# Second layer of a two-layer network on one core: score products of 64 rows placed in both row halves of the array in turn, with `center` held twice

## The chip, the cores and the metric

The kernel runs on one core of one Trainium2 chip. The metric is device time in microseconds (us), the median of several executions; lower is better. One more execution was taken with the hardware profiler on. It gives the span of the program (first to last instruction) and a trace of every instruction, and all start times below are counted from the start of that span.

The engines are named as in the profile: PE is the matrix engine and PEld its weight loads, DVE, ACT and POOL are the three engines for vectors, SP issues most of the DMAs. [...]

## What is computed

Four images of 512 channels and 32x32 pixels go through two layers, each with a residual. The first layer (group norm, layer norm, a selective scan, a projection) isn't touched by the change. The second is attention over positions and two 3x3 convolutions, on the group-normed image:

```python
def _L1_conv_ref(x, w_top, b_top, w_center, b_center, w_bottom, b_bottom, w_out, b_out):
    B, C, OUT_C, PAB, H, W = (4, 512, 512, 64, 64, 64)
    ...
    x_top = _conv(x, w_top, b_top, 0).reshape(bsz, -1, hw)          # 64 x 1024
    x_center = _conv(x, w_center, b_center, 0).reshape(bsz, -1, hw) # 64 x 1024
    x_bottom = _conv(x, w_bottom, b_bottom, 1).reshape(bsz, c, hw)  # 3x3, 512 -> 512
    ...
    sp_map = jnp.einsum('bnp,bpm->bnm', x_center, x_top)            # 1024 x 1024 scores, sum over 64
    sp_map = jax.nn.softmax(sp_map.reshape(bsz, -1), axis=1).reshape(bsz, hw, hw)
    sp_map = jnp.einsum('bnm,bmc->bnc', sp_map, x_bottom)
    sp_map = sp_map.reshape(bsz, c, h, w)
    return _conv(x + sp_map, w_out, b_out, 1)                       # 3x3, 512 -> 512

x = x + _L0_conv_ref(_gn(x), ...)
x = x + _L1_conv_ref(_gn(x), ...)
```

The softmax runs over all 1024 x 1024 scores of an image at once. What matters here is that a score is a sum over only 64 products (`PAB = 64`), half of the 128 rows that the array has.

## The kernel before

**Two parts.** The first layer takes the span up to about 1872 us; there an order written by hand (`Plan`) issues the instructions. In the second layer the instructions are traced in plain Python order, and the framework's scheduler then fixes an order on each engine, puts in the waits and hands out the buffers of a pool to its tiles. An engine works through its own list strictly in order, so an instruction that waits holds up everything behind it on that engine. The scheduler's order need not be the traced one: work traced later is put into gaps.

**The calls for each image.** The functions are called in this order (the loop at the end of the kernel): `scores(0)`; then for images 0 and 1: `conv3(b0)`, `attend(0)`, `scores(1)`, `conv3(b1)`, `attend(1)`; then `conv3(o0)`, `finish(0)`, `conv3(o1)`, `finish(1)`, `scores(2)`, and the same for images 2 and 3. So there are four calls of `scores`, and behind each comes the 3x3 convolution `conv3(b...)` (`x_bottom`) of the same image, and only behind that `attend`, which needs the softmax.

**`scores`** makes the scores and their exponentials for one image:

- `top` and `center` (128x1024, in SBUF, from the pool `fp` under tag `f4` with three buffers, shared with the output tiles `o` of `finish`) get zeros in their rows 64 to 127 by two POOL memsets (L1406, L1407).
- For each half `h` of the positions, four fp32 matmuls (L1411, tile `pt`, weights of `top` and `center` side by side) give 64 rows of `top` and, in rows 64 to 127, 64 rows of `center`. ACT writes `center` (64x512, one instruction, L1416) and then `top` (four instructions of 64x128, L1423, which also put the positions into the order of the convolution's tiles).
- For each of eight groups `m` of 128 positions, and each half `h`, one fp32 matmul (L1432, tile `psc`) of 128 rows, of which 64 are the zeros. The profile shows each fp32 matmul as two passes, each with a weight load, so a call has 16 matmuls and 32 passes. ACT copies each result into `st` (L1436), DVE takes the row maximum of each 128x1024 `st` (L1437).
- A maximum over everything: DVE `mp` (L1440), POOL `ma` across the partitions (L1442), DVE negates it (L1443). Then eight exponentials of 128x1024 on ACT, in place (L1446), and their sum `rp` on DVE (L1450).

**`conv3`** is a 3x3 convolution in a transformed form: six row points `p` in the pairs (1, 2), (3, 4), (0, 5), and for each of them four column points `q` in the order 2, 1, 0, 3. A product is four matmuls (eight passes, L1584) into one tile `m`; for `p = q = 1` a matmul with one row adds the bias (L1589). Its weights (1 MB, tile `uw`, three buffers `u`) come by an SP DMA (L1580). DVE makes the inputs `v` (`rr` by L1483, L1484, L1547, L1556; then four instructions, L1461 to L1464), with help of ACT (`e`, `f`, L1480) and POOL (L1481, L1543, L1544, L1553, L1554). For each `p`, ACT scales `m[2]` into `e` (L1592) and DVE combines `m[1]`, `m[0]` and `m[3]` with it (L1601, four instructions). Only then is a bank of PSUM free again.

**Banks of PSUM.** The pool `pm` (tag `m`) has five, used by the `m` tiles of `conv3`; the pool `ps` (tag `ps`) has three, used by `pt`, `psc`, `pat` (`attend`), and the transposes `po` of `finish`. So PE can run five `m` tiles ahead of ACT and DVE in `conv3`.

**`attend`** multiplies the exponentials with `x_bottom` (L1643, 128 matmuls per image) and adds the result to the image (DVE, L1658). For images 0 and 1, DVE also transforms pieces of the second convolution's weights there (L1508 to L1519).

The lines that the change touches are the first half of `scores`:

Of the kernel before, what the change touches and what calls it, by code (L numbers as in the profile page):

```python
# [8 lines left out]
F32 = mybir.dt.float32  # L9
AF = mybir.ActivationFunctionType  # L10
ALU = mybir.AluOpType
AX = mybir.AxisListType
# [3 lines left out]
P = 128  # L16
B, C, HH, WW = 4, 512, 32, 32
L = HH * WW
# [5 lines left out]
T = 512  # L24
NH = L // T
NB = B * NH
PAB = 64
# [4 lines left out]
    xp=(1, 2, 1),  # L32
# [184 lines left out]
def mamba_then_pab_kernel(  # L217
# [25 lines left out]
    nc = tc.nc  # L243
# [20 lines left out]
    pb_sb = cpool.tile([P, 1], F32, tag="pb", name="pb_sb")  # L264
# [58 lines left out]
    with ExitStack() as l0:  # L323
# [985 lines left out]
        for b in range(B):  # L1309
            at = b * NDC * NS  # L1310
            for n in range(NDC):
                e, h = divmod(n, NH)
# [30 lines left out]
    with ExitStack() as l1:  # L1343

        pm = l1.enter_context(tc.tile_pool(name="l1pm", bufs=5, space=PSUM))
        ps = l1.enter_context(tc.tile_pool(name="l1ps", bufs=3, space=PSUM))
        wp = l1.enter_context(tc.tile_pool(name="l1w", bufs=1))

        TI, TJ = HH // 4, WW // 2
# [6 lines left out]
        xp = l1.enter_context(tc.tile_pool(name="l1x", bufs=2))  # L1356
        fp = l1.enter_context(tc.tile_pool(name="l1f", bufs=3))

        NMC = L // P
# [40 lines left out]
        def scores(b, xg):  # L1400

            top = fp.tile([P, L], F32, tag="f4", name=f"top_{b}")
            center = fp.tile([P, L], F32, tag="f4", name=f"center_{b}")
            nc.gpsimd.memset(top[PAB:P, :], 0.0)  # L1406
            nc.gpsimd.memset(center[PAB:P, :], 0.0)  # L1407
            for h in range(NH):
                pt = ps.tile([P, T], F32, tag="ps", name=f"pt_{b}_{h}")
                for c in range(NCC):  # L1410
                    nc.tensor.matmul(  # L1411
                        pt, wt_sb[:, c].rearrange("p j n -> p (j n)"),
                        xg[:, c, 1 + h * HR : 1 + (h + 1) * HR, 1 : WW + 1],
                        start=(c == 0), stop=(c == NCC - 1),
                    )
                nc.scalar.activation(  # L1416
                    center[0:PAB, h * T : (h + 1) * T], pt[PAB:P], AF.Identity, bias=pb_sb[PAB:P]
                )
                tv = top[0:PAB].rearrange("p (r k i j) -> p r i j k", r=4, k=2, j=TJ)
                pv = pt[0:PAB].rearrange("p (i r j k) -> p r i j k", r=4, j=TJ, k=2)  # L1420
                hi = slice(h * TI // 2, (h + 1) * TI // 2)
                for r in range(4):
                    nc.scalar.activation(  # L1423
                        tv[:, r, hi], pv[:, r], AF.Identity, bias=pb_sb[0:PAB]
                    )
            mx = spool.tile([P, NMC], F32, tag="mx", name=f"mx_{b}")
            st = []
            for m in range(NMC):
                t = xp.tile([P, L], F32, tag="st", name=f"st_{b}_{m}", bufs=NMC)
                for h in range(NH):  # L1430
                    pt = ps.tile([P, T], F32, tag="ps", name=f"psc_{b}_{m}_{h}")
                    nc.tensor.matmul(  # L1432
                        pt, top[:, m * P : (m + 1) * P], center[:, h * T : (h + 1) * T],
                        start=True, stop=True,
                    )
                    nc.scalar.copy(t[:, h * T : (h + 1) * T], pt)  # L1436
                nc.vector.reduce_max(mx[:, m : m + 1], t, axis=AX.X)  # L1437
                st.append(t)
            mp = spool.tile([P, 1], F32, tag="mp", name=f"mp_{b}")
            nc.vector.reduce_max(mp, mx, axis=AX.X)  # L1440
            ma = spool.tile([P, 1], F32, tag="ma", name=f"ma_{b}")
            nc.gpsimd.partition_all_reduce(ma, mp, P, bass_isa.ReduceOp.max)  # L1442
            nc.vector.tensor_scalar_mul(ma, ma, -1.0)  # L1443
            rs = spool.tile([P, NMC], F32, tag="rs", name=f"rs_{b}")
            for m in range(NMC):
                nc.scalar.activation(  # L1446
                    st[m], st[m], AF.Exp, bias=ma, accum_out=rs[:, m : m + 1]
                )
            rp = spool.tile([P, 1], F32, tag="rp", name=f"rp_{b}")
            nc.vector.reduce_sum(rp, rs, axis=AX.X)  # L1450
            return st, rp
# [310 lines left out]
        left = list(range(EARLY, NPC))  # L1762
        half = len(left) // 2
        st, rp = scores(0, image[0])
        for a in range(0, B, 2):
            ins = None
            for b in (a, a + 1):
                xb = conv3(f"b{b}", image[b], ub, brow[0], behind=ins)
                also = left[b * half : (b + 1) * half] if not a else []
                after, v = iter(()), None  # L1770
                if b == a:
                    after = norm(b + 1)
                    next(after)
                    next(after)
                else:
                    v = first_inputs(f"o{a}", image[a])
                ins = attend(b, image[b], st, rp, xb, after, also)
                if b == a:
                    st, rp = scores(b + 1, image[b + 1])
            if a + 2 < B:  # L1780
                after = norm(a + 2, True)
                mid = lambda: next(after)
            else:
                mid = None
            y = conv3(f"o{a}", image[a], uo, brow[1], v, mid=mid)
            next(after, None)
            finish(a, y)
            if a + 2 == B:
                last(a + 1, image[a + 1], None)
                break  # L1790
            next(after, None)
            finish(a + 1, conv3(f"o{a + 1}", image[a + 1], uo, brow[1]))
            st, rp = scores(a + 2, image[a + 2])
# [57 lines left out]
```

## Time and profile before

| what | us |
|---|---|
| median of 3 executions | 2886.27 (2882.78 to 2889.2) |
| the profiled execution, device time | 2896.7 |
| the profiled execution, span | 2894.9 |
| outside the span (2896.7 - 2894.9) | 1.8 |
| second layer, from the first instruction of `scores(0)` to the end | about 1022 |
| `psc` matmuls, PE busy, all four calls (128 passes) | 55.8 |
| copies `st<-psc`, ACT busy, all four calls (64) | 37.5 |
| row maxima `mx<-st`, 32 of 1.22 us | 39.0 |
| memsets of `top` and `center`, POOL, 8 of 0.95 us | 7.6 |

The groups of the profile give busy time, the mean of one instruction, and the idle time of the engine just ahead of them with what ended it. The chain of waits is followed back from the last instruction: what stands in it set the end of the program, and work that does not stand in it was hidden. The timeline shows instructions in order of time, equal neighbours merged; in square brackets is the idle time ahead, and what ended it.

The four calls of `scores` lie at these times on PE (start of the first `pt`, start of the first `psc`, end of the last):

| call | first `pt` | first `psc` | last `psc` ends | what PE does between `pt` and `psc` |
|---|---|---|---|---|
| `scores(0)` | 1875.80 | 1886.98 | 1900.95 | idle for 1.31 us |
| `scores(1)` | 2043.59 | 2053.36 | 2067.26 | 4 passes of `m_b`, with 0.93 us idle ahead |
| `scores(2)` | 2392.40 | 2403.86 | 2417.86 | passes of `m_b` and the bias, no idle time |
| `scores(3)` | 2553.16 | 2561.77 | 2575.67 | 4 passes of `m_b`, no idle time |

### The profile page before, as it was taken

How to read it: one execution, taken by the hardware profiler on the slowest of the kernel's cores; microseconds unless marked ns; L12 is line 12 of the kernel's file. 1: busy time of each engine (PE TensorE's matmuls, PEld its weight loads, DVE VectorE, ACT ScalarE, POOL GpSimd, SP SyncE). 2: the span in 40 equal slices, each digit the busy share in tenths (PEclk: the TensorE clock that was granted, in tenths of full speed). 3: DMA queues.
4: the chain of work that ended last, by engine and by line, in shares of the span. 5: the costliest groups of instructions: out<-in, count | busy, mean ns of one | idle time of the engine just before them, and what ended most of it. 6: DMA issues, size and time to landing. Idle time of an engine off the chain costs nothing.

```text
span 2894.9 us, 36258 instructions
## 1 busy us (share of the span) xinstructions
PE 2720.9 (94%) x11752; PEld 1628.6 (56%) x11752; DVE 2288.4 (79%) x2730; ACT 1837.1 (63%) x3250; POOL 2039.3 (70%) x1243
## 2 busy tenths in 40 slices
PE   6898799999999999989989999899999999999999
PEld 2466566666666666666667766544444444444445
DVE  4579999989999889989899999867776755346264
ACT  4789999999899999899999999530300003030000
POOL 6999999899998999999999999733241341214222
PEclk9999999999999999999999999899999999999999
DMA  6766655567655577645565664757789886536586
GB/s 182 209 178 190 190 166 176 159 216 243 197 163 167 161 230 229 200 144 179 160 203 178 210 196 147 180 215 259 257 277 304 315 322 240 188 123 240 189 318 241
DMA packets 406548, 603.68 MB, mean 209 GB/s; under 512 B 47224, under 2 KB 246136, under 8 KB 382040
## 3 DMA queue, kind: packets, MB, share of 16 engines
q1 hardware_dynamic: 398744, 587.11, 63.6%
q10 hardware_dynamic: 7616, 14.26, 1.3%
q8 instruction: 94, 1.54, 0.2%
q14 instruction: 94, 0.77, 0.1%
HBM read 504.27 MB, written 96.99 MB: 208 GB/s over the span
## 4 chain that ended last, share of the span: by engine, by line
PE 44%; ACT 19%; DVE 15%; POOL 9%; issue 6%; DMA 5%; SPq 0%; POOLq 0%; DVEq 0%; ACTq 0%
PE m_o L1584 10%; PE m_b L1584 8%; DVE da L957 5%; ACT sc L917 4%; PE y L990 4%; PE pat L1643 4%; ACT da L904 4%; PE u L943 3%; POOL da L980 3%; PE pxm L444 3%; PE po L444 3%; ACT u L904 3%; PE pz L444 2%; DVE u L957 2%; PE pp L800 1%
## 5 line engine op out<-in xcount | busy, mean ns | idle before, releaser
L980 POOL TENSOR_TENSOR da<-da,cbc 128x1024 f32<-128x1024 f32 x314 | 741.6, 2368 | 33.3 <-DVE da L957 8.3
L917 ACT ACTIVATE sc<-dtxt,bt_sb 128x256 f32<-128x256 f32 x1256 | 550.7, 499 | 17.1 <-PE u L943 16.4
L932 POOL TENSOR_TENSOR dbx<-dtx,bbc 128x1024 f32<-128x1024 f32 x198 | 467.1, 2369 | 20.2 <-PE y L990 7.8
L904 ACT ACTIVATE da<-dt,a_sb 128x512 f32<-128x512 f32 x628 | 433.7, 714 | 15.4 <-PE y L990 10.6
L957 DVE TENSOR_TENSOR_SCAN da<-da,u 128x512 f32<-128x512 f32 x328 | 383.1, 1203 | 40.5 <-PE u L943 23.3
L943 PE MATMUL u<-ident,sc 128*128 128x128 f32 x2512 | 363.1, 279 | 33.4 <-DVE da L957 19.6
L943 PEld LDWEIGHTS u<-ident,sc 128*128 128x128 f32 x2512 | 291.6, 142 | 161.6 <-issue 47.2
L957 DVE TENSOR_TENSOR_SCAN da<-da,carry_sb,u 128x512 f32<-128x512 f32 x300 | 367.2, 1260 | 13.7 <-PE u L943 10.3
L990 PE MATMUL y<-ident,da 128*128 128x128 f32 x2512 | 339.5, 277 | 27.7 <-POOL da L980 27.0
L1584 PE MATMUL m_b<-uw_b,v_b 128*128 128x512 f32 x768 | 335.2, 596 | 6.7 <-DMA uw_b<-u_b 4.4
L990 PEld LDWEIGHTS y<-ident,da 128*128 128x128 f32 x2512 | 290.3, 142 | 90.2 <-POOL da L980 49.0
L1584 PE MATMUL m_o<-uw_o,v_o 128*128 128x512 f32 x736 | 321.9, 596 | 4.2 <-DMA uw_o<-u_o 4.1
L904 ACT ACTIVATE u<-dt,a_sb 128x512 f32<-128x512 f32 x396 | 262.5, 681 | 10.7 <-DVE da L957 5.8
L444 PE MATMUL pxm<-xt,winc 128*128 128x345 f32 (+3 forms) x704 | 242.7, 488 | 18.6 <-DVE xs L706 4.7
L1584 PEld LDWEIGHTS m_b<-uw_b,v_b 128*128 128x128 f32 x768 | 145.5, 191 | 192.9 <-issue 178.6
L444 PE MATMUL pz<-xt,winc 128*128 128x512 f32 x512 | 240.3, 600 | 2.1 <-ACT dtxt L881 1.0
L1584 PEld LDWEIGHTS m_o<-uw_o,v_o 128*128 128x128 f32 x736 | 139.0, 191 | 180.2 <-issue 173.2
L990 PE MATMUL y<-ident,dbx 128*128 128x128 f32 x1584 | 219.8, 276 | 12.2 <-DVE dbx L973 7.1
L980 POOL TENSOR_TENSOR dbx<-dbx,cbc 128x1024 f32<-128x1024 f32 x91 | 215.2, 2365 | 13.8 <-DVE dbx L957 7.0
L1643 PE MATMUL pat<-y_b,st 128*128 128x512 f32 x512 | 221.6, 593 | 1.7 <-DVE rz L1654 1.6
L990 PEld LDWEIGHTS y<-ident,dbx 128*128 128x128 f32 x1584 | 182.6, 142 | 48.4 <-issue 22.1
L444 PE MATMUL po<-gt,wpr 128*128 128x512 f32 x384 | 182.4, 594 | 4.3 <-DVE u L957 2.3
(231 smaller groups left out, 4113.2 us busy)
## 6 DMA issues: line engine op xcount, KB each, us to landing
cbc<-bcd SPq DMA_DIRECT2D x512, 256.0 KB, 3.6
uw_b<-u_b SPq DMA_DIRECT2D x96, 1024.0 KB, 4.8
uw_o<-u_o SPq DMA_DIRECT2D x92, 1024.0 KB, 4.8
bbc<-bcd SPq DMA_DIRECT2D x198, 256.0 KB, 4.1
u_b<-work SPq DMA_DIRECT2D x192, 128.0 KB, 2.7
winc<-in_w_in_dram SPq DMA_DIRECT2D x72, 256.0 KB, 3.6
szd<-sz SPq DMA_DIRECT2D x32, 512.0 KB, 3.7
szl<-szd SPq DMA_DIRECT2D x32, 512.0 KB, 5.0
```

What stands on the lines that cost most here:

```text
L444: lambda k=k, lhs=lhs, rhs=rhs: nc.tensor.matmul(p()[:, at : at + cols], lhs(), rhs(), start=(k == 0), stop=(k == n - 1)),
L800: lambda d=d, hs=hs, pp=pp: nc.tensor.matmul(pp()[p0 : p0 + NP, :], wx_sb[:, d, :], xs[b, d]()[:, hs], start=(d == 0), stop=(d == NDC - 1),),
L904: nc.scalar.activation(t, dt()[:, j], AF.Exp, scale=a_sb[:, at : at + 1])
L917: nc.scalar.activation(sc()[:, k], dtxt()[:, k], AF.Copy, scale=bt[:, at, s : s + 1])
L932: lambda: nc.gpsimd.tensor_mul(hc(), dtx(), b_bc().to_broadcast([P, 2, T])),
L943: nc.tensor.transpose(u()[:, k * P : (k + 1) * P], sc()[:, k, j, :], ident)
L957: nc.vector.tensor_tensor_scan(ht, *((hc()[:, j], u()) if on_act else (u(), hc()[:, j])), carry_sb[:, j, s : s + 1] if h else 0.0, ALU.mul ...
L980: nc.gpsimd.tensor_mul(hc(), hc(), c_bc().to_broadcast([P, 2, T]))
L990: nc.tensor.matmul(y[j]()[:, k, :], hc()[:, j, k * P : (k + 1) * P], ident, start=(s == 0 and k == 0), stop=(s == NS - 1 and k == NK - 1), ...
L1584: nc.tensor.matmul(m[q], v[:, q, k, c, :], w[:, c, :], start=(c == 0), stop=(c == NCC - 1 and not extra),)
L1643: nc.tensor.matmul(pt, st[m][:, 2 * P * j + h : 2 * P * (j + 1) : 2], xb[m // 2][:, m % 2, :], start=(m == 0), stop=(m == NMC - 1),)
```

## The change

All of it is in `scores`.

- The two memsets go.
- `top` is held without zeros: its groups `m` of even number lie in rows 0 to 63, those of odd number in rows 64 to 127. Two ACT instructions of 64x256 write it for each `h`, one for each row half, in place of four of 64x128.
- `center` is written twice, into rows 0 to 63 and into rows 64 to 127, each by an ACT instruction of 64x512, and both now stand behind the instructions for `top`.
- The score matmuls contract over 64 rows instead of 128. They are issued in pairs: group `g` with rows 0 to 63, then group `g + 1` with rows 64 to 127, first for `h = 0`, then for `h = 1`. The first of a pair writes into a bank of `ps`, the second into one of `pm`. Number of matmuls, columns and copies stay as they are.
- The copies follow a pair at a time, and the two row maxima of a pair come behind its four copies.

```diff
             center = fp.tile([P, L], F32, tag="f4", name=f"center_{b}")
-            nc.gpsimd.memset(top[PAB:P, :], 0.0)
-            nc.gpsimd.memset(center[PAB:P, :], 0.0)
             for h in range(NH):
...
-                nc.scalar.activation(
-                    center[0:PAB, h * T : (h + 1) * T], pt[PAB:P], AF.Identity, bias=pb_sb[PAB:P]
-                )
-                tv = top[0:PAB].rearrange("p (r k i j) -> p r i j k", r=4, k=2, j=TJ)
-                pv = pt[0:PAB].rearrange("p (i r j k) -> p r i j k", r=4, j=TJ, k=2)
+                pv = pt[0:PAB].rearrange("p (i r j k) -> p k r i j", r=4, j=TJ, k=2)
                 hi = slice(h * TI // 2, (h + 1) * TI // 2)
-                for r in range(4):
+                for k in range(2):
+                    tv = top[k * PAB : (k + 1) * PAB].rearrange(
+                        "p (r k i j) -> p k r i j", r=4, k=2, j=TJ
+                    )
                     nc.scalar.activation(
-                        tv[:, r, hi], pv[:, r], AF.Identity, bias=pb_sb[0:PAB]
+                        tv[:, k, :, hi], pv[:, k], AF.Identity, bias=pb_sb[0:PAB]
+                    )
+                for rows in (slice(0, PAB), slice(PAB, P)):
+                    nc.scalar.activation(
+                        center[rows, h * T : (h + 1) * T], pt[PAB:P], AF.Identity, bias=pb_sb[PAB:P]
                     )
             mx = spool.tile([P, NMC], F32, tag="mx", name=f"mx_{b}")
             st = []
-            for m in range(NMC):
-                t = xp.tile([P, L], F32, tag="st", name=f"st_{b}_{m}", bufs=NMC)
+            for g in range(0, NMC, 2):
+                two = [
+                    xp.tile([P, L], F32, tag="st", name=f"st_{b}_{g + k}", bufs=NMC) for k in range(2)
+                ]
                 for h in range(NH):
-                    pt = ps.tile([P, T], F32, tag="ps", name=f"psc_{b}_{m}_{h}")
-                    nc.tensor.matmul(
-                        pt, top[:, m * P : (m + 1) * P], center[:, h * T : (h + 1) * T],
-                        start=True, stop=True,
-                    )
-                    nc.scalar.copy(t[:, h * T : (h + 1) * T], pt)
-                nc.vector.reduce_max(mx[:, m : m + 1], t, axis=AX.X)
-                st.append(t)
+                    pts = [
+                        pool.tile([P, T], F32, tag=tag, name=f"psc_{b}_{g}_{h}_{tag}")
+                        for pool, tag in ((ps, "ps"), (pm, "m"))
+                    ]
+                    for k, pt in enumerate(pts):
+                        rows = slice(k * PAB, (k + 1) * PAB)
+                        nc.tensor.matmul(
+                            pt, top[rows, (g + k) * P : (g + k + 1) * P],
+                            center[rows, h * T : (h + 1) * T], start=True, stop=True,
+                        )
+                    for t, pt in zip(two, pts):
+                        nc.scalar.copy(t[:, h * T : (h + 1) * T], pt)
+                for k, t in enumerate(two):
+                    nc.vector.reduce_max(mx[:, g + k : g + k + 1], t, axis=AX.X)
+                st.extend(two)
```

## The prediction

> **What bounds the kernel now.** I read first the chain of waits from 1860 us to the end, to see where the score products (`psc`) set the end at all; then the timeline of PE at the four calls of `scores`; then ACT and DVE there, for what would become late next; last the groups, for prices.
>
> The chain of waits (start, us, what):
>
> ```profile
> 1886.98 13.97 PE psc L1432 x32
> ...
> 2068.80 2.24 DVE mx L1437 x2
> ...
> 2076.83 3.29 POOL e_o L1481
> 2080.11 2.48 POOL g_o L1543
> ...
> 2089.50 8.24 ACT st L1446 x15
> ...
> 2099.20 44.91 PE m_b L1584 x104
> ...
> 2403.93 13.93 PE psc L1432 x32
> ...
> 2597.26 8.89 ACT st L1446 x15
> ...
> 2606.95 51.77 PE m_b L1584 x120
> ```
>
> The `psc` matmuls stand in the chain in the first and the third call only. In the second and fourth the chain passes them by: it runs through DVE (inputs `rr`, `v` and row maxima), ACT and POOL (`e_o`, `g_o`), the maximum over partitions, the exponentials, and comes back to PE behind them. The timeline of PE shows the price of that:
>
> ```profile
> 1908.80 58.63 PE L1584 MATMUL m_b<-uw_b,v_b 128*128 128x512 f32 x136
> ...
> 2099.20 51.77 PE L1584 MATMUL m_b<-uw_b,v_b 128*128 128x512 f32 x120 [1.50 <-ACT e_b L1592]
> ...
> 2402.81 1.12 PE L1589 MATMUL m_b<-brow_b,ones 1*128 1x512 f32 x2
> 2403.86 14.00 PE L1432 MATMUL psc<-center,top 128*128 128x512 f32 x32
> ...
> 2606.95 51.77 PE L1584 MATMUL m_b<-uw_b,v_b 128*128 128x512 f32 x120 [0.85 <-ACT e_b L1592]
> ```
>
> Behind the second and fourth call PE stalls 1.50 and 0.85 us, all five banks of `pm` full, until ACT has done the exponentials and then the `e_b` of row point 2. Behind the first and third it runs on without a gap.
>
> **A pass, and what overlap would save.** 32 passes start over 13.73 us (13.93 in the chain, less the last one's tail): 0.429 us a pass. The trace has no two matmuls in different rows of the array in turn, so the gain has to be bounded. Nothing overlaps: 0. Full overlap: passes start in order, the second pass of one half runs with the first pass of the other, so 32 passes need 17 slots: 17 x 0.429 = 7.29 us, 6.44 less per call. A loss is bounded by the weight loads (0.19 us each, 186 ns in the loads of `psc`), if they could no longer run behind a pass: 32 x 0.19 = 6.1 us more. I take full overlap, because the two matmuls of a pair share no rows, operands or bank of PSUM; no row is near enough to choose a partial value.
>
> The nearest row for a change of the array's rows is the bias matmul (1 row). Its two passes start 1907.75, the next product at 1908.80; without a break they would be at 1907.66 and 1908.52. So one change into other rows costs 0.09 us and the way back 0.19, and the weights aren't loaded ahead there. I charge 0.19 for leaving `psc`; the entry is hidden in the first call's idle time, and in the third the bias has already to be left.
>
> [...]
>
> **Evictions.** Copies behind one another start 0.47 us apart: the two `e_b` at 2098.57 take 1.05 us together, one alone 0.58. Sixteen need 16 x 0.47 = 7.5 us, against 7.29 on PE: nearly the same pace. PE may be three pairs ahead (three banks in `ps`), and the last pair waits for the ninth copy, which ends 8 x 0.47 + 0.58 = 4.3 us behind the first one's start, before PE gets there (1.1 + 4.3 = 5.4 against 7 x 0.86 = 6.0 us). So ACT costs PE nothing; at 0.70 us a copy (`center` to `top` below, the widest row) it would cost 1.3 us a call.
>
> ```profile
> 1885.71 0.68 ACT L1416 ACTIVATE center<-pt,pb_sb 64x512 f32<-64x512 f32 x1 [1.51 <-PE pt L1411]
> 1886.41 1.24 ACT L1423 ACTIVATE top<-pt,pb_sb 64x128 f32<-64x128 f32 x4
> ```
>
> **Ahead of the products.** Now ACT takes `center` (next start 0.70 later), then four `top` (0.255 apart, (1.24 - 0.48) / 3): 1.7 us per half. Then it takes two `top` of 256 columns, about 0.40 apart (between the 0.255 of 128 and the 0.70 of 512), and two `center`: 2.2 us. The extra 0.5 us a half lies in ACT's idle time (1.44 and 1.51 us ahead of `center`). The first product needs only the first `top`: some 0.7 us behind `pt` instead of 1.31, 0.6 us won in the first call. In the others PE fills that time with `m_b`; if the bank order forbade that, the third call would lose up to 3.4 us (14.7 us from 2385 to the first product, less 4.4 of `po` and 6.9 of `pt`).
>
> **POOL and buffers.** Eight memsets go (7.6 us). POOL had waited 3.3 and 12.5 us in front of two of them, but its next work is the maximum over partitions, which waits for DVE's `mp` anyway (1911.34, 2419.77): worth 0. The wait for an `f4` buffer passes to ACT's first `top`; the buffers were free at 2393.8 and 2395.0, ACT comes at 2396.0, and only `psc` copies queue behind it. `psc` in `pm` adds a claim on five banks. At the third call two may still hold row point 1 (freed by 2393.3 and 2405.4); three suffice for the first pairs. Cost 0.
>
> **What is late next, call by call.**
>
> First: PE is offered 6.44 + 0.6 - 0.19 = 6.85 us. But DVE has no gap from 1894 to 1920, so `mp`, `ma` (1916.22) and the `n_b` behind it stay where they are.
>
> ```profile
> 1916.22 0.15 DVE L1443 TENSOR_SCALAR ma<-ma 128x1 f32<-128x1 f32 x1
> 1916.28 1.28 DVE L1601 SCALAR_TENSOR_TENSOR n_b<-m_b,e_b 128x512 f32<-128x512 f32 x2
> ```
>
> The seventh `m` tile (row point 2, `q = 0`) needs the bank that this `n_b` frees at 1917.56. It starts now at 1900.79 + 6 x 3.43 + 1.14 (bias) = 1922.5, 4.9 us later. So 4.9 of the 6.85 arrive and 2.0 become a wait. The next bound, `e_b` of row point 2 (done 1926.1, needed 1932.8), leaves 6.7.
>
> Second and fourth: DVE is without a gap from the end of `attend` to `mp` (2046 to 2078, 2553 to 2584) and is late with the row maxima by itself. Exponentials and `e_b` stay; PE arrives 6.2 us earlier and waits 6.2 us longer. Worth 0.
>
> Third: DVE waits 0.50 us for `st` ahead of nearly every row maximum, so here it follows: first pair copied at 2407, eight maxima of 1.15, `mp` near 2416.4 instead of 2419.8, exponentials over near 2431.5. PE needs that bank at 2441.7 - 6.25 = 2435.4. All of 6.44 - 0.19 = 6.25 arrives. Behind the first and third call the chain goes on through weights (`uw`, `wt`) that are loaded when PE frees a buffer, so they move with it.
>
> **Sum:** 4.9 + 0 + 6.25 + 0 = 11.1 us. The profiled execution (2896.7, of which 1.8 outside the span) becomes 2885.6; it lies 10.4 above the median, so on the median 2886.3 - 11.1 = **2875.2 us**.
>
> **Rivals.**
>
> - *The order on DVE and ACT moves too.* The scheduler makes it anew. If the row maxima come in a block ahead of the inputs, or `e_b` ahead of the exponentials, the gain arrives in all calls: 2.0 more in the first, 6.25 + 1.50 in the second, 6.25 + 0.85 in the fourth: 28 us, 2858.3. For it: ACT idles 11.27 and 12.37 us ahead of those exponentials. Against: the change orders none of this.
> - *The halves don't overlap* (or the change doesn't do what it says). Passes stay 0.429 apart; 0.6 won, twice 0.19 lost: 2886.1. For it: no row shows an overlap.
> [...]
>
> **Chances.** Forecast 0.45, order moved 0.15, no overlap 0.17, drain at each turn (or an order that turned out worse) 0.23. A measurement can't tell changes under about 0.2%, 5.8 us. So faster 0.60, same 0.17, slower 0.23. The likeliest case by itself runs from 2870 to 2880 (overlap of 0.77 to full, 3.4 lost in the third call, ACT at its widest). The range for all goes from 2857 to 2902: the whole of the first rival, the second, and the third up to its price at 0.28 a turn.
>
> **What would show it.** Passes of `psc` near 0.215 us apart in the mean, a call over within 7.3 to 9 us; PE starting some 0.7 us behind `pt`; a new wait of about 2 us for `n_b` near 1915; stalls for `e_b` (L1592) of 7 to 8 us behind the second and fourth call, with `mp` no earlier against the end of `attend`. Wrong would be: passes at 0.43 or more; no stall at those two places (first rival); the weight loads of `psc` no longer beside the matmuls (third).

## The result, and the profile after

| | before | after |
|---|---|---|
| median | 2887.73 (2882.78 to 2896.85, 4 executions) | 2873.08 (2868.84 to 2875.64, 4 executions) |
| profiled execution, device time | 2896.7 | 2872.42 |
| profiled execution, span | 2894.9 | 2870.6 |

The ratio is 0.9939, 95% interval [0.9924, 0.9954]: 0.61% or some 17.6 us faster (the two medians lie 14.7 apart). The forecast was 11.1 us. The time came out within 2.1 us of 2875.2, but that is in good part luck: the parts did not come where the forecast had them.

To compare kernels part by part I use the length of a *stage* on PE: from the first `pt` of a call of `scores` to the first `pat` of the same image (in the third call from the `po` transposes just ahead of `pt`). Whole spans are less sharp, since the first layer, which nothing here touches, ended anywhere from 1865.9 to 1875.8 us in the profiled executions.

| stage | before | after | after, second profile | gained | forecast |
|---|---|---|---|---|---|
| first call | 110.5 | 103.7 | 106.6 | 6.8 / 3.9 | 4.9 |
| second call | 107.2 | 99.5 | 99.5 | 7.7 / 7.7 | 0 |
| third call | 112.3 | 111.9 | 111.5 | 0.4 / 0.8 | 6.25 |
| fourth call | 105.4 | 99.5 | 99.6 | 5.9 / 5.8 | 0 |

**PE, after**: the timeline, as start, us, engine, line, operation, tile, shapes, number of instructions.

```profile
1882.91 0.69 PE L1440 MATMUL psc_ps<-center,top 64*128 64x512 f32 x1 [0.56 <-ACT top L1420]
1883.40 0.69 PE L1440 MATMUL psc_m<-center,top 64*128 64x512 f32 x1
...
1884.82 0.69 PE L1440 MATMUL psc_m<-center,top 64*128 64x512 f32 x1
...
1885.35 0.59 PE L1440 MATMUL psc_m<-center,top 64*128 64x512 f32 x1
...
1886.36 0.59 PE L1440 MATMUL psc_ps<-center,top 64*128 64x512 f32 x1
1886.64 0.59 PE L1440 MATMUL psc_m<-center,top 64*128 64x512 f32 x1
1886.79 0.59 PE L1440 MATMUL psc_ps<-center,top 64*128 64x512 f32 x1
...
1891.02 7.13 PE L1594 MATMUL m_b<-uw_b,v_b 128*128 128x512 f32 x16
...
1899.14 58.63 PE L1594 MATMUL m_b<-uw_b,v_b 128*128 128x512 f32 x136
...
2058.27 75.80 PE L1594 MATMUL m_b<-uw_b,v_b 128*128 128x512 f32 x176
...
2557.59 75.80 PE L1594 MATMUL m_b<-uw_b,v_b 128*128 128x512 f32 x176
```

Passes of one half start 0.43 us apart (1886.36, 1886.79), and a pass of the other half starts between them: the halves overlap. The whole call lasts 1891.02 - 1882.91 = 8.11 us, against 13.8 before (8.11 or 8.12 in all four calls). Behind the second and the fourth call PE now runs 75.80 us without a gap: the stalls for `e_b` (1.50 and 0.85 us) that were to grow to 7 or 8 us are gone.

**POOL, before**, the timeline around the second maximum over partitions:

```profile
2076.83 3.29 POOL L1481 TENSOR_TENSOR e_o<-e_o,xg 128x1088 f32<-128x1088 f32 x1 [19.80 <-ACT e_o L1480]
2080.05 2.54 POOL L1543 TENSOR_TENSOR g_o<-xg 128x1088 f32<-128x1088 f32 x1
2088.84 0.38 POOL L1442 PARTITION_ALL_REDUCE ma<-mp  x1 [6.25 <-issue]
```

and the group of its four maxima (busy time, mean ns; idle time ahead of them, and what ended it):

```profile
L1442 POOL PARTITION_ALL_REDUCE ma<-mp x4 | 4.6, 1139 | 29.5 <-issue 19.8 <-DVE mp L1440 9.7
```

**POOL, after**, the same two views:

```profile
2067.52 1.30 POOL L1452 PARTITION_ALL_REDUCE ma<-mp  x1 [19.92 <-DVE mp L1450]
2077.70 2.29 POOL L1491 TENSOR_TENSOR e_o<-e_o,xg 128x1088 f32<-128x1088 f32 x1 [8.88 <-ACT st L1456]
```

```profile
L1452 POOL PARTITION_ALL_REDUCE ma<-mp x4 | 4.2, 1056 | 76.9 <-DVE mp L1450 76.9
```

Before, DVE made `mp` at 2077.85, but POOL first did `e_o` and `g_o`, and then stood 6.25 us with nothing that the profile shows it waiting for ("issue"). In three of the four calls 19.8 us went that way (6.25, 6.18 and 7.36). After, the maximum stands ahead of `e_o` on POOL. Its idle time (8.20 to 28.77 us) ends with `mp` each time, and "issue" is gone from the group. I call those 6.2 to 7.4 us the *preparation* of the maximum; what POOL does in them no view shows. My reading is that after the change it lies inside a wait that is there anyway. From `mp` to the negated `ma` it took 4.9, 11.4, 5.75 and 12.5 us before, and 1.6, 1.6, 0.7 and 1.7 after.

**The third call, after**, the timeline of PE:

```profile
2368.50 0.77 PE L1692 MATMUL po<-ident,y_o 128*128 128x128 f32 x5 [0.93 <-POOL y_o L1616]
2369.76 2.28 PE L1692 MATMUL po<-ident,y_o 128*128 128x128 f32 x16 [0.50 <-DVE o L1697]
2372.08 3.68 PE L1409 MATMUL pt<-xg,wt_sb 128*128 128x512 f32 x8
2378.37 5.37 PE L1409 MATMUL pt<-xg,wt_sb 128*128 128x512 f32 x8 [2.61 <-DVE o L1697]
2384.30 0.69 PE L1440 MATMUL psc_ps<-center,top 64*128 64x512 f32 x1 [0.56 <-ACT top L1420]
```

and **before**, at the same place:

```profile
2386.36 1.02 PE L1584 MATMUL m_b<-uw_b,v_b 128*128 128x512 f32 x2
...
2388.51 1.88 PE L1584 MATMUL m_b<-uw_b,v_b 128*128 128x512 f32 x4
...
2391.54 1.02 PE L1584 MATMUL m_b<-uw_b,v_b 128*128 128x512 f32 x2
...
2395.84 2.73 PE L1584 MATMUL m_b<-uw_b,v_b 128*128 128x512 f32 x6
...
2401.86 1.02 PE L1584 MATMUL m_b<-uw_b,v_b 128*128 128x512 f32 x2
```

Before, 16 passes of `m_b` (and two of the bias) filled the time in which `po` and `pt` wait for DVE. After, none of them stands there: PE idles 0.93, 0.50, 2.61 and 0.56 us, and the second half of `pt` takes 5.37 us for the same eight passes. The windows show the clock that goes with it (us, then busy time of PE, PEld, DVE, ACT, POOL, the granted clock, the DMA share, GB/s):

```profile
2372.00:2378.40 6.40, 3.75 (x10) 1.49 (x9) 5.40 (x7) 2.30 (x4) 0.00 (x0) 1.00 0.64 238
2378.40:2384.30 5.90, 5.34 (x8) 1.94 (x9) 2.89 (x4) 0.50 (x2) 0.00 (x0) 0.71 0.22 89
```

Behind the idle time the granted clock is 0.71 for 5.9 us. The idle time alone doesn't bring that about: in e1, e4, e5 and e8 below, PE idles 2.65, 2.66, 2.58 and 2.46 us at this place, and the same eight passes take 3.68 or 3.69 us. Of the profiles with such a gap only the two of the changed kernel itself show 5.37 us (the gap is 2.35 us in the second). So 1.7 us of this stage (5.37 - 3.68) hang on something besides the length of the gap; what it is stays open.

### The profile page after: what moved, and what is told of

Read it like the earlier page. It is cut to its first block, busy times and chain, and to the rows that moved or that the text cites. A ratio compares the mean times of both kernels' runs of the same rounds, so it can differ in the third digit from the quotient of the medians.

```text
span 2870.6 us, 36232 instructions
## 1 busy us (share of the span) xinstructions
PE 2694.7 (94%) x11752; PEld 1619.5 (56%) x11752; DVE 2291.2 (80%) x2730; ACT 1835.4 (64%) x3242; POOL 2035.5 (71%) x1235
## 4 chain that ended last, share of the span: by engine, by line
PE 49%; ACT 18%; DVE 13%; POOL 8%; issue 6%; DMA 5%; SPq 0%; DVEq 0%; POOLq 0%; ACTq 0%
PE m_b L1594 11%; PE m_o L1594 10%; PE pat L1653 6%; DVE da L957 5%; PE y L990 4%; ACT sc L917 4%; POOL da L980 4%; PE u L943 4%; ACT da L904 3%; PE po L444 3%; ACT u L904 3%; PE pz L444 2%; PE pxm L444 2%; DVE u L957 2%; ACT L251 2%
## 5 line engine op out<-in xcount | busy, mean ns | idle before, releaser
L957 DVE TENSOR_TENSOR_SCAN da<-da,u 128x512 f32<-128x512 f32 x328 | 383.2, 1203 | 41.8 <-PE u L943 25.0
L943 PE MATMUL u<-ident,sc 128*128 128x128 f32 x2512 | 362.8, 279 | 33.4 <-DVE da L957 19.8
```

Source lines behind the costliest of these rows:

```text
L943: nc.tensor.transpose(u()[:, k * P : (k + 1) * P], sc()[:, k, j, :], ident)
L957: nc.vector.tensor_tensor_scan(ht, *((hc()[:, j], u()) if on_act else (u(), hc()[:, j])), carry_sb[:, j, s : s + 1] if h else 0.0, ALU.mul ...
```

## The experiments

Three things could have made the gain: the overlap of the halves, the maximum's place on POOL, and the missing memsets. The first four kernels were timed beside the kernel before (2889.65, 19 executions), the other four beside it again (2888.66, 17 executions).

**e1: the change without the overlap.** All groups of `top` in rows 0 to 63; order, banks and everything else as changed.

```diff
-                    tv = top[k * PAB : (k + 1) * PAB].rearrange(
+                    tv = top[0:PAB].rearrange(
...
-                        rows = slice(k * PAB, (k + 1) * PAB)
+                        rows = slice(0, PAB)
```

> The changed kernel with both matmuls of a pair in rows 0 to 63 (top of all groups written there), so that nothing can overlap; memsets gone, pairs, banks and the order of ACT, DVE and POOL as in the changed kernel. The stages are counted on PE from the first pt (third: from the first of the transposes po just ahead of it) to the first pat of the same image: 110.5, 107.2, 112.3, 105.4 us before, 103.7, 99.5, 111.9, 99.5 in the changed kernel. Theory (the overlap is what pays, and the softmax on DVE, POOL and ACT being early enough is what lets it through): passes 0.43 us apart, psc 13.7 us a call, every stage 5.6 to 6.4 us longer than in the changed kernel, that is about 110, 106, 118, 106; the time 22 to 25 us over the changed kernel, at or above the one before. Rival (stages two and four gained from the earlier maximum on POOL and the missing memsets, whatever PE does): those two stages stay within 2 us of 99.5, and the time is about 10 us over the changed kernel.

Measured: 2892.86 (2887.91 to 2895.45, 12 executions), ratio 1.0007 [0.9997, 1.0017]. Stages 108.5, 105.3, 115.9, 105.3. The timeline of PE:

```profile
1880.14 1.02 PE L1440 MATMUL psc_ps<-center,top 64*128 64x512 f32 x2
1881.00 1.02 PE L1440 MATMUL psc_m<-center,top 64*128 64x512 f32 x2
```

Two passes of one tile, then two of the next, 0.86 us a matmul: without the second row half nothing overlaps, and a call takes 13.93 us. The time is 19.8 us above that of the changed kernel, somewhat less than the 22 to 25 expected. Half the rows alone are worth nothing, and the early maximum alone (`mp` to `ma` 1.6 us here as well) takes 1.9 us off the second stage and 0.1 off the fourth. The overlap is what the net gain hangs on.

**e2: both tiles of a pair from `ps`.** Three banks for `psc` instead of one from each of two pools.

```diff
-                        pool.tile([P, T], F32, tag=tag, name=f"psc_{b}_{g}_{h}_{tag}")
-                        for pool, tag in ((ps, "ps"), (pm, "m"))
+                        ps.tile([P, T], F32, tag="ps", name=f"psc_{b}_{g}_{h}_{k}")
+                        for k in range(2)
```

> The changed kernel with both tiles of a pair in the pool ps (three banks) and none in pm. Theory (in the third call the products' claim on pm keeps the m tiles of conv3, traced later, from going ahead of them, and PE idles and its clock drops): work of conv3 stands ahead of psc again in the third call, that stage falls from 111.9 to about 106.5; in all calls PE is at most one and a half pairs ahead of ACT, psc ends about 1 us later, first, second and fourth stage up to 1 us longer; sum 1 to 4 us below the changed kernel. Rival (the third call lost its gain for another reason, the waits for the transposes and the output loads): that stage stays at 111 to 112 and the time is 2 to 4 us above the changed kernel.

Measured: 2872.55 (6 executions), ratio 0.9938 [0.9923, 0.9954]; stages 106.2, 102.0, 107.0, 102.2. The third stage falls by 4.9 us against the changed kernel (111.9): with `psc` out of `pm`, products of `m_b` stand ahead of it again. But a call of `psc` takes 10.0 to 10.75 us instead of 8.11, which I put down to the three banks in all, with which PE can be only one and a half pairs ahead of ACT's copies; I had put that at 1 us, and it costs 2.5 and 2.7 in the second and the fourth stage. Gain and loss cancel, where 1 to 4 us had been expected.

**e3: only the third call takes both tiles from `ps`.**

```diff
-                        for pool, tag in ((ps, "ps"), (pm, "m"))
+                        for pool, tag in ((ps, "ps"), (ps, "ps") if b == 2 else (pm, "m"))
```

> The changed kernel, with ps alone used for psc in the third call only (image 2), pm as well in the other three. Theory as for the kernel with ps alone: third stage about 106.5, the other three at 103.7, 99.5, 99.5 as in the changed kernel; time 4 to 6 us below the changed kernel. Rival: third stage 111 to 112, time the same as the changed kernel.

Measured: 2868.18 (2862.83 to 2870.06, 6 executions), ratio 0.9918 [0.9903, 0.9933]; stages 107.1, 99.7, 107.0, 99.5. PE ahead of the third call's products:

```profile
2370.10 1.02 PE L1594 MATMUL m_b<-uw_b,v_b 128*128 128x512 f32 x2
...
2379.57 2.74 PE L1594 MATMUL m_b<-uw_b,v_b 128*128 128x512 f32 x6
2382.16 3.71 PE L1409 MATMUL pt<-xg,wt_sb 128*128 128x512 f32 x8
```

The filler is back and the eight passes of `pt` take 3.71 us again instead of 5.37. The third stage's loss is therefore the bank. A reading that fits is that `psc` in `pm` is handed its bank in traced order, ahead of the convolution's tiles, so that those can't be put in front of it; the handing out itself is not to be seen in a trace. The first stage, 107.1 where 103.7 was expected, is taken up under e6.

**e4: the maximum late on POOL.** A copy ahead of the maximum, so that other POOL work stands between the preparation and the maximum's wait again.

```diff
+            nc.gpsimd.tensor_copy(ma, mx[:, NMC - 1 : NMC])
             nc.gpsimd.partition_all_reduce(
```

> The changed kernel with one small POOL copy of the last column of mx into ma put in front of the maximum across partitions, so that POOL can reach the maximum only behind the last row maximum. Theory (POOL needs about 6 us of preparation for that instruction, which the changed kernel hides because POOL idles ahead of it, and the kernel before did not, because a memset or the convolution's inputs stood in front): the time from mp to ma grows from 1.5 us to 5 to 7 us in all four calls, PE stalls for e_b or n_b behind calls one, two and four by 2 to 4 us each, the time 5 to 11 us over the changed kernel. Rival (the maximum simply takes 1.3 us, and before it was late only because of what stood in front): ma within 0.5 us of the changed kernel's, time the same.

Measured: 2881.76 (8 executions), ratio 0.9965 [0.9951, 0.9978]; stages 108.2, 103.7, 110.3, 105.6; `mp` to `ma` 8.4, 6.6, 7.6 and 9.6 us. POOL and PE at the second call:

```profile
2066.11 1.18 POOL L1452 COPY ma<-mx 128x1 f32<-128x1 f32 x1 [18.57 <-DVE mx L1447]
2073.38 0.38 POOL L1453 PARTITION_ALL_REDUCE ma<-mp  x1 [6.09 <-issue]
...
2083.73 17.43 PE L1595 MATMUL m_b<-uw_b,v_b 128*128 128x512 f32 x40 [1.50 <-ACT e_b L1603]
2103.37 26.88 PE L1595 MATMUL m_b<-uw_b,v_b 128*128 128x512 f32 x62 [2.20 <-DVE n_b L1612]
```

The 6.09 us of preparation are exposed again (7.00 and 9.00 in the third and fourth call), and PE stalls for `e_b` and then for `n_b`. From `mp` to `ma` it is more than the 5 to 7 us expected in three of the four calls. One small instruction on POOL takes back 4.2 and 6.1 us of the second and fourth stage, and about half of the whole gain.

**e5: the memsets back.** The changed kernel with the two POOL memsets.

```diff
+            nc.gpsimd.memset(top[PAB:P, :], 0.0)
+            nc.gpsimd.memset(center[PAB:P, :], 0.0)
             for h in range(NH):
```

> The changed kernel with the two POOL memsets put back ahead of `pt` (they now only delay ACT's writes of the upper rows and stand in POOL's queue). My theory: a memset that waits on POOL for the end of the score products of the call before matters only where it stands directly ahead of the maximum over partitions; the first maximum of a pair of images may come 2 to 6 us later, but ACT's copies and DVE's products cover that. Stages from the first `pt` to the first `pat`: 104, 100, 112 to 114, 100 us (each within 2 us of the changed kernel); `mp` to `ma` under 3 us in the second and fourth call, up to 7 us in the third; time within 3 us of the changed kernel, ratio to before 0.993 to 0.995. Rival: the memsets were what exposed the preparation of the maximum in all calls; then `mp` to `ma` is 5 us or more in at least three calls and the time is 5 us or more above that of the changed kernel.

Measured: 2874.56 (2870.31 to 2881.75, 6 executions), ratio 0.9952 [0.9938, 0.9966]; stages 108.4, 99.7, 110.8, 99.5; `mp` to `ma` 4.9, 1.6, 4.4 and 1.6 us. The median is 3.2 us above e6, a little over the 3 us expected, with overlapping intervals; the first stage (108.4) missed the 104 by 4 us, and e6 and e7 show why that stage scatters. POOL in the third call:

```profile
2391.71 0.95 POOL L1407 MEMSET center<- 64x1024 f32 x1 [7.98 <-PE psc_m L1442]
2398.74 0.38 POOL L1454 PARTITION_ALL_REDUCE ma<-mp  x1 [6.08 <-issue]
```

In the third call the memset stands directly ahead of the maximum and its preparation is exposed, yet the stage (110.8) is at most 0.6 us longer for it, if the changed kernel's 111.9 is taken without the 1.7 us of its slow passes; in the first the maximum itself is recorded with 3.43 us instead of 1.24. The rival (three or more calls at 5 us) falls.

**e6: the changed kernel again**, unaltered, for a direct comparison.

> The changed kernel itself, unaltered, in the same call as the others, so that they can be compared with it directly. Expected: ratio to before 0.992 to 0.996, stages 104, 100, 112, 100 us, each within 1.5 us; the first layer's end may lie anywhere from 1867 to 1876 us, as it did in kernels that leave it alone.

Measured: 2871.39 (2867.68 to 2872.52, 5 executions), ratio 0.9936 [0.9924, 0.9948]; stages 106.6, 99.5, 111.5, 99.6. The first stage is 2.9 us longer than in the first profile of the same program, and outside the 1.5 us expected. PE and DVE of e6 there:

```profile
1909.62 44.90 PE L1594 MATMUL m_b<-uw_b,v_b 128*128 128x512 f32 x104 [2.85 <-DVE n_b L1611]
...
1881.23 1.23 DVE L1471 TENSOR_TENSOR v_b<-rr_b 128x1024 f32<-128x1024 f32 x1
1882.37 3.57 DVE L1472 TENSOR_TENSOR v_b<-rr_b 128x1024 f32<-128x1024 f32 x1
1885.85 3.59 DVE L1473 TENSOR_TENSOR v_b<-rr_b 128x1024 f32<-128x1024 f32 x1
...
1881.34 3.51 POOL L1563 TENSOR_TENSOR l_b<-xg 128x1088 f32<-128x1088 f32 x1 [2.49 <-DVE rr_b L1494]
1884.81 3.54 POOL L1564 TENSOR_TENSOR k_b<-xg 128x1088 f32<-128x1088 f32 x1
```

and of the first profile of the same kernel, with an `l_b` of the third image last, beside which DVE makes no such additions:

```profile
1887.61 1.25 DVE L1471 TENSOR_TENSOR v_b<-rr_b 128x1024 f32<-128x1024 f32 x1
1888.75 1.25 DVE L1472 TENSOR_TENSOR v_b<-rr_b 128x1024 f32<-128x1024 f32 x1
1889.88 1.25 DVE L1473 TENSOR_TENSOR v_b<-rr_b 128x1024 f32<-128x1024 f32 x1
...
1887.72 5.82 POOL L1563 TENSOR_TENSOR l_b<-xg 128x1088 f32<-128x1088 f32 x1 [2.49 <-DVE rr_b L1494]
...
2323.76 2.54 POOL L1563 TENSOR_TENSOR l_b<-xg 128x1088 f32<-128x1088 f32 x1 [4.96 <-DVE rr_b L1494]
```

Same instructions, same order, and in both DVE's first addition (L1471) starts 0.11 us ahead of `l_b`. In e6 both are then longer: `l_b` and `k_b` take 1.0 us more than the 2.54 of an `l_b` by itself, and DVE's next two additions 2.3 us more each, as if the two took turns; I call this pattern turns. In the other execution DVE does three additions in 1.25 us each, and `l_b` takes 3.3 us more. Eight of the ten profiled executions, the one before the change among them, show the turns of e6 (`l_b` of 3.5 us); only the first profile of the changed kernel and e8 show the other pattern. In e6 `n_b` comes late, and the wait that the forecast had put near 1915 (2.0 us) is there, with 2.85 us.

So in both executions some of the instructions that run side by side on DVE and POOL take longer: in e6 two additions (3.57 and 3.59 us instead of 1.25), `l_b` and `k_b`, in the other `l_b` (5.82 us instead of 2.54). What decides between the two patterns the rows don't show: DVE starts first by 0.11 us in both, and the second addition takes 3.57 us in e6 and 1.25 us in the other.

**e7: e3 again**, beside e6.

> The version in which only the third call takes both banks of a pair from `ps`, unaltered, beside the changed kernel. My theory: the third stage is 107 us again instead of 112, because the products of the convolution stand ahead of the score products again, at a cost of 2.4 us in them; the first is 107 instead of 104, because of the wait for `n_b`. Second and fourth as in the changed kernel. Sum of the four stages 413 to 414 against 414 to 415: time 1 to 5 us below the changed kernel. Rival: the gain of the third call is given back in the first, and what was measured before (4.9 us) was the spread of the first layer; then the two medians lie within 1.5 us.

Measured: 2865.57 (2861.18 to 2872.77, 6 executions), ratio 0.9921 [0.9907, 0.9935]; stages 108.8, 99.8, 106.2, 99.5. The median is 5.8 us below e6, slightly more than the 1 to 5 expected; e3 was 4.9 below the first result of the changed kernel. The sum of its stages (414.3) lies 2.9 below that of e6 (417.2). The third stage is the steady part of it, 106.2 and 107.0 against 111.5 and 111.9; in the first stage POOL took its turns both times, as in e6, with waits of 1.77 and 1.81 us for `n_b`. (The first stage of e7, 108.8 where 107 was expected, has besides 40 passes that take 19.10 us, against 17.74 in e3.) The intervals of the ratios of e6 and e7 overlap, so the size of the advantage isn't settled; the lower median and the shorter third stage came out both times.

**e8: nothing but the pairs.** The kernel before, 128 rows and memsets as they were, with matmuls, copies and maxima in pairs and the second tile in `pm`.

```diff
-            for m in range(NMC):
+            for g in range(0, NMC, 2):
...
+                        for pool, tag in ((ps, "ps"), (pm, "m"))
...
+                            pt, top[:, (g + k) * P : (g + k + 1) * P],
+                            center[:, h * T : (h + 1) * T], start=True, stop=True,
```

> The kernel before with nothing of the change but the order in pairs and the second bank: both products of a pair over all 128 rows, zeros by the two memsets, entry as before. Theory: score products 13.7 to 14 us a call; the maximum over partitions stands on POOL ahead of the inputs of the second convolution again, so `mp` to `ma` falls below 2.5 us in the second and fourth call and their stages come to 105 to 106 us without the stall for `e_b`; third stage 114 to 119 us, because the bank of `pm` keeps the convolution's products behind the score products. Time equal to before within 6 us. Rival: the early maximum came from the missing memsets; then `mp` to `ma` stays above 8 us in the second and fourth call and the stalls of 0.8 to 1.5 us are there.

Measured: 2895.18 (2889.88 to 2900.08, 12 executions), ratio 1.0021 [1.0012, 1.0030], so slower by 6.5 us in the medians, just over the 6 expected. `mp` to `ma` is 1.6 us in the second and fourth call (4.9 and 6.5 in the first and third, where a memset stands ahead of the maximum), stages 110.6, 105.9, 118.3, 105.8, the third 6.0 longer than before. POOL in the second call and PE in the third:

```profile
2072.51 1.30 POOL L1450 PARTITION_ALL_REDUCE ma<-mp  x1 [19.95 <-DVE mp L1448]
...
2390.18 3.68 PE L1411 MATMUL pt<-xg,wt_sb 128*128 128x512 f32 x8 [2.46 <-DVE o L1695]
```

So pairs with their second tile in `pm` bring both by-products without overlap: the maximum moves to the front on POOL, and the third call loses its filler. e2 tells the two causes apart: with both tiles in `ps` the maximum is as early (1.6 us in the second and fourth call) and the filler stays. The early maximum goes with the order in pairs, the lost filler with the bank. The rival (the missing memsets moved the maximum) falls.

## Why the prediction was right in the sum and wrong in its parts

That the sum came close is luck. The second and fourth call were put at 0 and gave 7.7 and 5.9 us; the third was put at 6.25 and gave 0.4 to 0.8.

**Overlap of the row halves: right.** Forecast 7.29 us a call, measured 8.11. Most of the missing 0.8 us goes in the first two pairs: in the first call the second tile's first matmul starts at 1883.40 and its next at 1884.82, 1.42 us later, where later ones follow 0.86 apart, and the two passes of that next one start 0.53 apart (1884.82, 1885.35) instead of 0.43. The group of its weight loads in the profile after (busy time, mean ns; idle time ahead, and what ended it) names ACT's last writes of `center` and `top`:

```profile
L1440 PEld LDWEIGHTS psc_m<-center,top 64*128 64x128 f32 x64 | 11.3, 186 | 7.8 <-issue 2.9 <-ACT center L1424 1.7 <-ACT top L1420 0.8
```

The loads stay beside the matmuls, at 186 ns in the mean against 190 before. A turn between the halves then costs nothing here: a pass of each half fits into the 0.43 us of one. Leaving for the convolution costs 0.09 us instead of 0.19: the last pass starts 0.43 behind 1890.07, and the next product 0.52 behind that. The rival with no overlap falls. No run shows two terms that the forecast's range and chances reckon with, an overlap of 0.77 and a loss at each turn between the halves (2902 is its price at 0.28 us a turn): measured were 13.74 - 8.11 = 5.6 of the bound of 6.44 us, 0.87 of it, and turns without a loss.

**Entry and copies: right.** PE idles 0.56 us instead of 1.31 ahead of the first call (forecast 0.7); copies behind one another start 0.478 us apart (forecast 0.47).

**First call: right in kind, with a spread.** The step "`mp`, `ma` and the `n_b` behind it stay where they are" held for `mp` and `n_b` where POOL took its turns, as in the profile that the forecast was made from: in e6 they were done 36.1 and 42.4 us behind the first `pt` against 35.7 and 41.8 before (`ma` came some 3 us sooner), the stage gained 3.9 us, and the wait for `n_b` was 2.85 us (1.77 and 1.81 in e3 and e7). In the result's own profile POOL was held up instead (`l_b` 5.82 us), DVE was early, and 6.8 us came. One number for this stage was too sharp for what two executions of the same program show.

**Second and fourth call: wrong.** The failing step reads "Exponentials and `e_b` stay; PE arrives 6.2 us earlier and waits 6.2 us longer. Worth 0." `mp` indeed hardly moved (34.3 us behind the first `pt` before, 32.8 after, in the second call), but the exponentials did, since POOL's maximum came 9.8 us sooner behind it. I had seen `e_o` and `g_o` in the chain of waits just ahead of the maximum, and took their order as given. What arrives is close to the sum of its parts. Second call: 13.74 - 8.11 = 5.6 from the products, 1.50 from the stall, 0.93 of idle time ahead of the filler that is gone, less the 0.56 now ahead of the products: 7.5, measured 7.7. Fourth: 5.6 + 0.85 - 0.56 = 5.9, measured 5.9. The rival "the order on DVE and ACT moves too" had 7.75 and 7.1 there, and its sign, no stall at those two places, is what came; but the engine whose order moved was POOL. Neither part does it alone:

| second / fourth stage | maximum late | maximum early |
|---|---|---|
| no overlap | 107.2 / 105.4 (before) | 105.3 / 105.3 (e1), 105.9 / 105.8 (e8) |
| overlap | 103.7 / 105.6 (e4) | 99.5 / 99.5 (after) |

In the fourth call the forecast's "worth 0" is what e4 measured (105.6 against 105.4); in the second 3.5 us arrived with a maximum that is late, though less late than before (6.6 us instead of 11.4).

**Third call: the loss was named and mis-sized.** The forecast said that a bank order that forbids the filler "would lose up to 3.4 us (14.7 us from 2385 to the first product, ...)". The first number was a slip: from 2385.16 to 2403.86 are 18.7 us, and less 4.4 and 6.9 that bounds the loss at 7.4. I also took "Cost 0" for the claim on `pm`, having looked at when banks come free and not at the order in which they are handed out. Measured: the third stage of e3 and e7 is 5.1 us shorter than that of the changed kernel (means 106.6 and 111.7), although their products take 2.4 us longer: 7.5 us. Against it stand 13.84 - 8.11 = 5.7 from the products and 2.3 from further on, where a wait for weights became shorter (0.9) and slow passes were missing (1.5): before, PE waited 2.17 us for `uw` at 2478.41, and its 40 passes behind it took 19.10 us at a granted clock of 0.69 in the first 5.6; after, it waits 0.69 and 0.60 and 40 passes take 17.6. The sum, 0.5, fits the measured 0.4 to 0.8. But slow passes count on both sides (1.7 us behind the gap at `pt` after, 1.5 us before), and e1, e4, e5 and e8 have the same gap at `pt` without them; without them the bank would cost 5.8 us in place of 7.5.

**Memsets: right for the time, wrong in the reason.** "Its next work is the maximum over partitions, which waits for DVE's `mp` anyway" overlooked the preparation, which came behind what stood in front on POOL. e5 shows it exposed in the third call (6.08 us behind the memset), and the stage at most 0.6 us longer for it.

What stays open: why the scheduler puts the maximum ahead of `e_o` once the products come in pairs. Of the change, e2 and e8 have only the order in pairs in common, and e5 and e8 show that the memsets are not it; which of its rules decides was not tried.

## What to carry to other kernels

Products over 64 rows placed in both row halves in turn, into separate banks, ran at twice the pace here (0.86 us for two matmuls instead of 1.72); order the entry so that both halves have their data at once. Before pricing a stage at zero because an engine further on is late, look at what that engine's lateness is made of: here 10 us of it were an accident of order, and a change that orders nothing there removed them. A tile moved into another pool can keep that pool's later work from being put ahead of it (here 16 passes); ask what that work was filling.

## What the runs showed that I had not expected

- A maximum over partitions on POOL whose busy time is 0.38 us stood 5.8 to 9.0 us without a visible reason in eight places where other POOL work was directly ahead of it (6.25, 6.18, 7.36 before; 6.09, 7.00, 9.00 in e4; 6.08 in e5; 5.79 in e8). In the changed kernel, where POOL waits 8.20 to 28.77 us for `mp`, no such time shows.
- PE idle for 2.61 us was followed by a granted clock of 0.71 over 5.9 us, and eight passes took 5.37 us instead of 3.68. The length of the gap doesn't decide it: behind 2.46 to 2.66 us at the same place in four other kernels the passes kept their pace, and behind 2.85 us elsewhere in e6 104 passes took 44.90 us, 0.43 each.
- The same additions on DVE took 1.25 or 3.57 us in two executions of one program, beside an `l_b` on POOL of 5.82 us in the first and of 3.51 us in the second.
